# Layer norms of the second batch and of the s branch moved in small pieces into the attention loop, first projections put between the first norms

## The chip, the cores and the metric

The kernel runs on one core of one Trainium2 chip, in one launch. The metric is the device time of that launch in microseconds, the median of several runs. All tensors are float32. Engine names are those of the profile: PE is TensorE (PEld its weight loads), DVE is VectorE, ACT is ScalarE, POOL is GpSimd, SP is SyncE. ACT and SP also issue DMAs here (ACTq and SPq).

## The reference, cut to what matters

The input x has two batches of 2048 tokens with 256 features. It is normalised once, and the result xn goes into two branches: s, an attention over all 2048 tokens with 16 heads of 16, to which a second layer norm of xn is added; and g, two layers of windowed attention with a gated feed-forward. The output is x + s * silu(ffn(xn)).

```python
xn = _layernorm(x)                        # no weights: (x - mean) / sqrt(var + 1e-5)
# s branch
q, k, v = split(xn @ W_qkv.T)             # 16 heads of 16
attn = softmax(q @ k.T * scale + spatial_bias)    # bias on tokens 1..256 only
s = (attn @ v) @ W_proj.T + b_proj + _layernorm(xn) * ln_gamma + ln_beta
# spatial_bias: -0.1 * dist / max(dist) over 256 centres
g = silu(ffn(xn))                         # depth 2, windows of 128 tokens
out = x + s * g
```

## The kernel before

The program runs in three stages, one after the other: `norms`, `global_attention`, `ffn_branch`.

`norms` goes through eight chunks of 512 tokens, four to a batch, each held as four tiles of 128 tokens by 256 features. For each chunk it loads x (SP), takes mean and variance of each tile with a BATCH_NORM_STATS and a BATCH_NORM_AGGREGATE instruction (L92 and L93, DVE), takes the root on ACT (L95) and the reciprocal on DVE (L96), and writes the normalised tiles to `xn` (L106, four TENSOR_SCALAR). TensorE transposes the chunk into two banks `pt` (L112) and ACT copies them to `xA[b]` (L113), the transposed activations that all later projections read. Then the same statistics are taken of `xn`, and the result is written to `s_all` (L117, DVE), multiplied by gamma (L120, POOL) and increased by beta plus b_proj (L121, POOL). `s_all` is the accumulator of s; the attention adds its output to it.

`spatial_bias` computes the bias of 257 rows from the centres: five small DVE operations and a root on ACT for each of three row groups, a maximum over all partitions on POOL (L158), and a scaling (L160 to L166).

`global_attention` is written in manual order: every engine executes its instructions in the order in which the program emits them. The 4 groups of 4 heads, 2 batches and 4 query chunks make 32 units. Three kinds of pieces run through PE:

- P pieces (`max_piece`, L280): the scores of 128 queries against 512 keys for one head, of which DVE takes only the maximum (L283, `mx`).
- S pieces (`score_piece`, L316): the scores transposed, with the maximum already subtracted through an added row; ACT takes the exponential (L322). In the first query chunk of a group (qc == 0) DVE adds the bias to the first 257 rows (L320).
- V pieces (`sum_piece`, L335): the sums of exponentials times values; ACT copies the bank out (L344), POOL adds it to the running sum `o` (L345).

P pieces and V sums take their PSUM banks from a ring of four (`p`), S pieces and everything else from another ring of four (`s`). The written order of one period, four key tiles of one unit, is the list `PATTERN`; in it X stands for one piece of other work: the next group's projections (`prep_qk` L232, `prep_v` L247), the `augment` of a unit (L293), or the closing steps of a unit (`sums` L352, `normalize` L364, `project` L374). A unit has four periods; the loop runs 130 of them.

Before the loop, the projections of the first group run as one block (13 pieces of `prep_pieces(0)`), and then 80 P pieces alone (the lead), since the maxima of a whole unit have to be known before its first S piece. Each P piece in the lead needs one DVE maximum.

`ffn_branch` has its own pools and starts when the attention is done. It is not touched.

DMA order: SP issues the x chunks and the centres; ACT issues the weights wq, wk, wv, wp, ones and the three rows ln_gamma, ln_beta, b_proj. DMAs share eight completion semaphores in turn; an issue waits until the previous DMA on its semaphore has landed.

Of the kernel before, what the change touches and what calls it, by code (L numbers as in the profile page):

```python
# [11 lines left out]
F32 = mybir.dt.float32  # L12
# [6 lines left out]
P = 128  # L19
NT = N // P  # L20
CH = 512
# [16 lines left out]
def gated_recurrent_kernel(ctx: ExitStack, tc: tile.TileContext, t: dict, out: bass.AP):  # L38
# [28 lines left out]
    with tc.tile_pool(name="s", bufs=1) as sp:  # L67
        s_all = sp.tile([P, B * NT, D], F32, name="s_all")
        norms(tc, t, xA, s_all, ident, eps_t, x_ch)
        global_attention(tc, t, xA, s_all, s_out, ident)  # L70
# [3 lines left out]
def norms(tc, t, xA, s_all, ident, eps_t, x_ch):  # L74

    nc = tc.nc
    with tc.tile_pool(name="ln", bufs=2) as lp, tc.tile_pool(name="ln1", bufs=1) as lp1, tc.tile_pool(
        name="ln_ps", bufs=4, space=PSUM
    ) as lps:
        gam = lp1.tile([P, D], F32, name="gam")  # L80
        nc.scalar.dma_start(gam, t["ln_gamma"][None, :].to_broadcast([P, D]))
        bet = lp1.tile([P, D], F32, name="bet")
        nc.scalar.dma_start(bet, t["ln_beta"][None, :].to_broadcast([P, D]))
        bpr = lp1.tile([P, D], F32, name="bpr")
        nc.scalar.dma_start(bpr, t["b_proj"][None, :].to_broadcast([P, D]))
        nc.vector.tensor_add(bet, bet, bpr)

        def stats(src, c, tag):
            mv = lp.tile([P, TPC, 2], F32, tag=f"mv{tag}", name=f"mv{tag}_{c}")
            for i in range(TPC):  # L90
                st = lp.tile([P, 6], F32, tag=f"st{tag}", name=f"st{tag}_{c}_{i}", bufs=4)
                nc.vector.bn_stats(st, src[:, i, :])  # L92
                nc.vector.bn_aggr(mv[:, i, :], st)  # L93
            rs = lp.tile([P, TPC], F32, tag=f"rs{tag}", name=f"rs{tag}_{c}")
            nc.scalar.activation(rs, mv[:, :, 1], AF.Sqrt, bias=eps_t)  # L95
            nc.vector.reciprocal(rs, rs)  # L96
            return mv, rs

        for c in range(B * NCH):
            b, cc = divmod(c, NCH)  # L100
            xt = lp.tile([P, TPC, D], F32, tag="xt", name=f"xt_{c}", bufs=3)
            nc.sync.dma_start(xt, x_ch[c])
            mv, rs = stats(xt, c, "a")
            xn = lp.tile([P, TPC, D], F32, tag="xn", name=f"xn_{c}")
            for i in range(TPC):
                nc.vector.tensor_scalar(  # L106
                    xn[:, i, :], xt[:, i, :], mv[:, i, 0:1], rs[:, i : i + 1], ALU.subtract, ALU.mult
                )
            for k in range(2):
                pt = lps.tile([P, CH], F32, tag="pt", name=f"pt_{c}_{k}")  # L110
                for i in range(TPC):
                    nc.tensor.transpose(pt[:, i * P : (i + 1) * P], xn[:, i, k * P : (k + 1) * P], ident)  # L112
                nc.scalar.copy(xA[b][:, k, 1 + cc * CH : 1 + (cc + 1) * CH], pt)  # L113
            mv, rs = stats(xn, c, "b")
            sl = s_all[:, c * TPC : (c + 1) * TPC, :]
            for i in range(TPC):
                nc.vector.tensor_scalar(  # L117
                    sl[:, i, :], xn[:, i, :], mv[:, i, 0:1], rs[:, i : i + 1], ALU.subtract, ALU.mult
                )
            nc.gpsimd.tensor_mul(sl, sl, gam[:, None, :].to_broadcast([P, TPC, D]))  # L120
            nc.gpsimd.tensor_add(sl, sl, bet[:, None, :].to_broadcast([P, TPC, D]))  # L121


def spatial_bias(tc, t, pool):


    nc = tc.nc
    bias = pool.tile([P, 2, NC_SP], F32, name="bias")
    bias_last = pool.tile([1, NC_SP], F32, name="bias_last")
    with tc.tile_pool(name="sb", bufs=1) as sp:  # L130
        cb = sp.tile([P, NC_SP, 2], F32, name="cb")
        nc.sync.dma_start(
            cb.rearrange("p n c -> p (n c)"),
            t["centers"].rearrange("n c -> (n c)")[None, :].to_broadcast([P, 2 * NC_SP]),
        )
        cp = sp.tile([P, 3, 2], F32, name="cp")
        nc.gpsimd.memset(cp, 0.0)
        nc.sync.dma_start(cp[1:P, 0, :], t["centers"][0 : P - 1, :])
        nc.sync.dma_start(cp[:, 1, :], t["centers"][P - 1 : 2 * P - 1, :])
        nc.sync.dma_start(cp[0:1, 2, :], t["centers"][2 * P - 1 : 2 * P, :])  # L140
        dy = sp.tile([P, NC_SP], F32, name="dy")
        for kt in range(3):
            rows = P if kt < 2 else 1
            d = bias[:, kt, :] if kt < 2 else bias_last
            nc.vector.tensor_scalar(d, cb[:rows, :, 0], cp[:rows, kt, 0:1], None, ALU.subtract)
            nc.vector.tensor_mul(d, d, d)
            nc.vector.tensor_scalar(dy[:rows], cb[:rows, :, 1], cp[:rows, kt, 1:2], None, ALU.subtract)
            nc.vector.tensor_mul(dy[:rows], dy[:rows], dy[:rows])
            nc.vector.tensor_add(d, d, dy[:rows])
            nc.scalar.activation(d, d, AF.Sqrt)  # L150
        nc.vector.memset(bias[0:1, 0, :], 0.0)
        mx = sp.tile([P, 1], F32, name="mx")
        nc.vector.tensor_reduce(mx, bias.rearrange("p k n -> p (k n)"), AX.X, ALU.max)
        mx1 = sp.tile([1, 1], F32, name="mx1")
        nc.vector.tensor_reduce(mx1, bias_last, AX.X, ALU.max)
        nc.vector.tensor_max(mx[0:1], mx[0:1], mx1)
        mxa = sp.tile([P, 1], F32, name="mxa")
        nc.gpsimd.partition_all_reduce(mxa, mx, P, ReduceOp.max)  # L158
        on = sp.tile([P, 1], F32, name="on")
        nc.vector.tensor_scalar(on, mxa, 1e-6, -0.1, ALU.is_gt, ALU.mult)  # L160
        co = sp.tile([P, 1], F32, name="co")
        nc.vector.tensor_scalar_max(co, mxa, 1e-6)
        nc.vector.reciprocal(co, co)
        nc.vector.tensor_mul(co, co, on)
        nc.vector.tensor_scalar_mul(bias, bias, co)
        nc.vector.tensor_scalar_mul(bias_last, bias_last, co[0:1])  # L166
    return bias, bias_last
# [5 lines left out]
    "S0 S3 P1 P2 S0 P3 V V P2 P0 S3 S1 P1 P0 S3 S2 P1 S0 S2 P3 X P3 P0 S1 S2 X S1 P0 P2 S3 S1 S0 P2 P3 V V P1 S2"  # L173
# [7 lines left out]
def global_attention(tc, t, xA, s_all, s_out, ident):  # L181
# [6 lines left out]
    with ExitStack() as ctx:  # L188
        cp = ctx.enter_context(tc.tile_pool(name="ga_c", bufs=1))
        bias, bias_last = spatial_bias(tc, t, cp)  # L190
# [12 lines left out]
        negm = [cp.tile([P, TPC * GH, HP], F32, name=f"negm{i}") for i in range(2)]  # L203
        for m in negm:
            nc.gpsimd.memset(m, 0.0)
        ctx.enter_context(tc.manual_schedule())

        units = [(b, g, qc) for b in range(B) for g in range(NG) for qc in range(NCH)]
        groups = [(b, g) for b in range(B) for g in range(NG)]
# [779 lines left out]
```

## Time and profile before

| what | value |
|---|---|
| median of 3 runs | 3884.55 us (3881.63 to 3889.24) |
| profiled execution | 3884.26 us, of which the span is 3882.5 us |
| busy in the span | PE 92%, DVE 60%, ACT 53%, POOL 30% |
| first P piece starts | 118.03 us |
| first maximum of the lead (L283) starts | 119.19 us |
| end of the lead, first S piece (L316) starts | 176.59 us |
| one unit of the loop | 59.1 us (59.16 us from 793.57 to 852.73) |
| DMA | mean 10 GB/s over the span |

The page gives one execution, in microseconds from the start of the span. "Busy tenths" are 40 equal slices of 97 us. The chain is the sequence of work that ended last, followed back from the end. Matmul rows count each float32 matmul twice, since it is done in two passes with a weight load each.

### The profile page before, as it was taken

What the parts mean: (1) busy time and instruction counts of PE and PEld (TensorE: products, weight loads), DVE (VectorE), ACT (ScalarE), POOL (GpSimd) and SP (SyncE); (2) the same over time, 40 slices, a digit from 0 to 9 for tenths busy, and PEclk for the clock granted to TensorE, in tenths of its full rate; (3) what the DMA queues carried; (4) which work ended last, traced back from release to release, by engine and by line L of the source; (5) the groups of instructions that cost most, each with busy time, mean ns of one, the idle gap of its engine ahead of it and who ended that gap; (6) DMA issues with size and microseconds to landing.
All of it is one profiled execution on the core that took longest, in us unless ns stands there. A gap on an engine that the chain in (4) does not pass through costs nothing.

```text
span 3882.5 us, 56277 instructions
## 1 busy us (share of the span) xinstructions
PE 3564.7 (92%) x21856; PEld 1688.3 (43%) x21856; DVE 2334.0 (60%) x4894; ACT 2063.8 (53%) x4170; POOL 1156.3 (30%) x978
## 2 busy tenths in 40 slices
PE   2999999999999999999996778888989999999998
PEld 1534334334343343434432444444444445555554
DVE  8767777777777777777751444545444444444442
ACT  1166666666666666666663344444444444444452
POOL 4011111111111111111113544445444435454441
PEclk9699999999999999999997899999999999999999
DMA  2000000000000000000002000000000000000001
GB/s 72 4 1 1 1 1 1 1 1 1 12 6 7 1 1 1 1 1 1 1 12 79 1 6 1 6 1 6 1 22 6 1 28 9 17 17 17 17 9 44
DMA packets 26172, 40.44 MB, mean 10 GB/s; under 512 B 3806, under 2 KB 19122, under 8 KB 25906
## 3 DMA queue, kind: packets, MB, share of 16 engines
q1 hardware_dynamic: 24466, 34.08, 2.6%
q8 instruction: 172, 2.82, 0.3%
q10 hardware_dynamic: 1440, 2.77, 0.2%
q14 instruction: 94, 0.77, 0.1%
HBM read 28.46 MB, written 8.39 MB: 9 GB/s over the span
## 4 chain that ended last, share of the span: by engine, by line
PE 76%; DVE 11%; ACT 5%; POOL 5%; issue 2%; DMA 1%; ACTq 0%; POOLq 0%; SPq 0%; DVEq 0%
PE pm L280 16%; PE po L335 12%; PE ps L316 11%; PE pg L757 7%; PE pp L552 6%; PE po L689 4%; DVE mx L283 3%; PE px L704 3%; PE pz L800 2%; POOL sm L654 2%; PE pw L668 2%; PE px L374 2%; PE pt L598 2%; ACT sm L645 2%; PE pp_wk L232 2%
## 5 line engine op out<-in xcount | busy, mean ns | idle before, releaser
L283 DVE TENSOR_REDUCE mx<-pm 128x1 f32<-128x512 f32 x2048 | 1285.6, 683 | 450.9 <-PE ps L316 429.9
L322 ACT ACTIVATE e<-ps 128x512 f32<-128x512 f32 x2048 | 1059.4, 607 | 466.2 <-PE ps L316 345.0
L280 PE MATMUL pm<-kT,qT 32*128 32x512 f32 x4096 | 1148.8, 639 | 0.8 <-DVE mx L283 0.8
L316 PE MATMUL ps<-qa,kT 32*128 32x512 f32 x4096 | 1116.5, 627 | 5.7 <-ACT e L322 4.8
L345 POOL TENSOR_TENSOR o<-o,part 128x512 f32<-128x512 f32 x224 | 283.5, 1266 | 1580.6 <-ACT part L344 1580.6
L280 PEld LDWEIGHTS pm<-kT,qT 32*128 32x128 f32 x4096 | 432.4, 188 | 435.4 <-DVE mx L283 338.5
L335 PE MATMUL po<-e,v 128*32 128x512 f32 x4096 | 492.5, 598 | 0.0
L316 PEld LDWEIGHTS ps<-qa,kT 32*128 32x128 f32 x4096 | 390.9, 183 | 154.6 <-ACT e L322 62.5
L576 POOL TENSOR_TENSOR rot<-rot,swp 128x512 f32<-128x512 f32 x128 | 162.4, 1269 | 797.5 <-DVE swp L575 757.7
L552 PE MATMUL pp<-wqkv,xA 128*128 128x512 f32 x768 | 379.9, 618 | 14.4 <-DMA wqkv<-in_wqkv_dram 14.4
L757 PE MATMUL pg<-hc,w 128*128 128x512 f32 (+1 forms) x768 | 379.8, 629 | 0.0
L645 ACT ACTIVATE sm<-sm,wmx 128x256 f32<-128x256 f32 (+1 forms) x512 | 250.4, 490 | 171.9 <-DVE wmx L636 171.2
L654 POOL TENSOR_TENSOR sm<-sm,wls 128x512 f32<-128x512 f32 (+1 forms) x256 | 254.2, 1014 | 26.6 <-DVE wls L651 23.7
L335 PEld LDWEIGHTS po<-e,v 128*32 128x32 f32 x4096 | 106.9, 109 | 348.1 <-DVE mx L283 187.4
L573 DVE TENSOR_TENSOR rot<-pp,rt 128x512 f32<-128x512 f32 x128 | 88.5, 691 | 248.7 <-ACT sqq L567 230.4
L585 POOL TENSOR_TENSOR rn<-rn,mhalf 128x8 f32<-128x8 f32 x128 | 210.8, 1647 | 55.4 <-DVE rn L584 55.4
L344 ACT COPY part<-po 128x512 f32<-128x512 f32 x224 | 131.0, 585 | 167.0 <-PE po L335 167.0
L689 PE MATMUL po<-pT,v 128*64 128x128 f32 x1984 | 159.3, 301 | 55.8 <-DVE pT L675 55.8
L552 PEld LDWEIGHTS pp<-wqkv,xA 128*128 128x128 f32 x768 | 138.7, 197 | 154.3 <-issue 141.2
L668 PE MATMUL pw<-ident,sm 128*128 128x128 f32 x992 | 150.0, 288 | 60.6 <-POOL sm L654 59.7
L675 DVE COPY pT<-pw 128x512 f32<-128x512 f32 (+1 forms) x128 | 84.8, 672 | 195.5 <-PE pw L668 195.4
L757 PEld LDWEIGHTS pg<-hc,w 128*128 128x128 f32 (+1 forms) x768 | 132.9, 187 | 142.0 <-issue 141.3
(136 smaller groups left out, 3795.8 us busy)
## 6 DMA issues: line engine op xcount, KB each, us to landing
xt<-in_x_dram SPq DMA_DIRECT2D x8, 512.0 KB, 3.7
s_out<-s_all SPq DMA_DIRECT2D x8, 512.0 KB, 2.6
rt<-in_rot_dram SPq DMA_DIRECT2D x16, 256.0 KB, 4.6
s<-s_out SPq DMA_DIRECT2D x16, 256.0 KB, 3.4
x<-in_x_dram SPq DMA_DIRECT2D x16, 256.0 KB, 3.5
out_dram<-y SPq DMA_DIRECT2D x16, 256.0 KB, 2.2
wqkv<-in_wqkv_dram SPq DMA_DIRECT2D x4, 768.0 KB, 8.3
w<-in_w_dram SPq DMA_DIRECT2D x4, 682.0 KB, 5.5
```

The costliest lines, as they stand in the source:

```text
L280: nc.tensor.matmul(ps, qT[rows, q0 : q0 + P], kT[rows, c * CH : (c + 1) * CH], start=True, stop=True)
L283: nc.vector.tensor_reduce(mxs[n][:, i * GH + j, c : c + 1], ps, AX.X, ALU.max)
L316: nc.tensor.matmul(ps, kT[rows, kt * P : (kt + 1) * P], qas[n][rows, :], start=True, stop=True)
L322: nc.scalar.activation(e, ps, AF.Exp)
L335: nc.tensor.matmul(pos[n][j * HP : (j + 1) * HP, :], v[:, kt, j * HP : (j + 1) * HP], es.pop((n, kt, j)), start=(kt % 2 == 0), stop=(kt % ...
L345: nc.gpsimd.tensor_add(os[n], os[n], part)
L552: nc.tensor.matmul(ps, xA[b][:, k, at : at + P], W["qkv"][:, k, n * INNER : (n + 1) * INNER], start=(k == 0), stop=(k == 1),)
L645: nc.scalar.activation(sm[:, x, lo:], sm[:, x, lo:], AF.Exp, scale=-1.0, bias=mx[:, hb, r, x : x + 1], accum_out=ls[:, hb, r, x : x + 1],)
L654: nc.gpsimd.tensor_mul(sm, sm, ls[:, hb, r, :, None].to_broadcast([P, 2, 2 * P - lo]))
L668: nc.tensor.transpose(ps[:, x, pa, :], S["sm"][hb, r][:, x, pa * P : (pa + 1) * P], ident)
L689: nc.tensor.matmul(S["po"][r * HD2 : (r + 1) * HD2, c, :], kvs[l, b, kt, "v"][:, h * HD2 : (h + 1) * HD2], S["pT", hb, r][:, x, pa, :], st ...
L757: nc.tensor.matmul(ps[:mw], W["1"][:, k, at : at + mw], hc[:, k, :], start=(k == 0), stop=(k == 1))
```

## The change

The function `norms` is gone, and its work is in `global_attention` as pieces.

1. Batch 0's first norm: load, statistics, root (still on ACT), application and transposes of a chunk are emitted chunk by chunk before the loop. Between them stand a step of `spatial_bias`, now a generator that yields between its steps, and the projections of group 0 for the chunk before (`prep_qk` for wk and wq, then `prep_v`). The rest of `spatial_bias` and the addition of b_proj to beta follow after the last projection and before the lead.
2. The norm of s (`s_pieces`) and batch 1's first norm (`xn_pieces` of chunks 4 to 7) are split into 80 pieces in the list `aside`, in the order: s of batch 0 (24 pieces), xn of batch 1 (32), s of batch 1 (24). A new letter N in `PATTERN`, three times a period, executes one of them. N stands after the first V pair, after the first X, and after the second V pair.
3. In the loop the inverse root is a power on POOL (`inv_std`, an add and a pow of 128x4). The normalised tile is written into `s_all` itself, the transposes read it there (`turn_over`), and the norm of s is done in place by two SCALAR_TENSOR_TENSOR instructions of DVE for each tile, which contain gamma and beta. The two POOL instructions of a chunk (L120, L121) are gone.
4. wq, wk, wv, wp and ones are issued at the start of the program, before gamma, beta and b_proj. x has two buffers in place of three; the temporaries of `spatial_bias` share the buffers of `e`.

```diff
-        norms(tc, t, xA, s_all, ident, eps_t, x_ch)
-        global_attention(tc, t, xA, s_all, s_out, ident)
+        global_attention(tc, t, xA, s_all, s_out, ident, eps_t, x_ch)
...
-            mv, rs = stats(xn, c, "b")
-            sl = s_all[:, c * TPC : (c + 1) * TPC, :]
-            for i in range(TPC):
-                nc.vector.tensor_scalar(
-                    sl[:, i, :], xn[:, i, :], mv[:, i, 0:1], rs[:, i : i + 1], ALU.subtract, ALU.mult
-                )
-            nc.gpsimd.tensor_mul(sl, sl, gam[:, None, :].to_broadcast([P, TPC, D]))
-            nc.gpsimd.tensor_add(sl, sl, bet[:, None, :].to_broadcast([P, TPC, D]))
...
-    "S0 S3 P1 P2 S0 P3 V V P2 P0 S3 S1 P1 P0 S3 S2 P1 S0 S2 P3 X P3 P0 S1 S2 X S1 P0 P2 S3 S1 S0 P2 P3 V V P1 S2"
+    "S0 S3 P1 P2 S0 P3 V V N P2 P0 S3 S1 P1 P0 S3 S2 P1 S0 S2 P3 X N P3 P0 S1 S2 X S1 P0 P2 S3 S1 S0 P2 P3 V V N P1 S2"
...
+        def stats(src, mv, tiles):
+            for i in tiles:
+                st = p2.tile([P, 6], F32, tag="st", name="st", bufs=4)
+                nc.vector.bn_stats(st, src[:, i, :])
+                nc.vector.bn_aggr(mv[:, i, :], st)
+
+        def inv_std(mv, rs):
+            nc.gpsimd.tensor_add(rs, mv[:, :, 1], ep4)
+            nc.gpsimd.tensor_tensor(rs, rs, mhalf, ALU.pow)
...
+            def root():
+                if b:
+                    inv_std(h["mv"], h["rs"])
+                else:
+                    nc.scalar.activation(h["rs"], h["mv"][:, :, 1], AF.Sqrt, bias=eps_t)
+                    nc.vector.reciprocal(h["rs"], h["rs"])
+
+            def apply(tiles):
+                for i in tiles:
+                    nc.vector.tensor_scalar(
+                        sl[:, i, :], h["x"][:, i, :], h["mv"][:, i, 0:1], h["rs"][:, i : i + 1],
+                        ALU.subtract, ALU.mult,
+                    )
+
+            def turn_over(k):
+                pt = bank(f"pt_{c}_{k}")
+                for i in range(TPC):
+                    nc.tensor.transpose(pt[:, i * P : (i + 1) * P], sl[:, i, k * P : (k + 1) * P], ident)
+                nc.scalar.copy(xA[b][:, k, 1 + cc * CH : 1 + (cc + 1) * CH], pt)
+
+            return [
+                load, lambda: stats(h["x"], h["mv"], (0, 1)), lambda: stats(h["x"], h["mv"], (2, 3)), root,
+                lambda: apply((0, 1)), lambda: apply((2, 3)),
+            ], [lambda: turn_over(0), lambda: turn_over(1)]
...
+            def first():
...
+                stats(sl, h["mv"], (0, 1))
+
+            def rest():
+                stats(sl, h["mv"], (2, 3))
+                inv_std(h["mv"], h["rs"])
+
+            def apply(i):
+                x = sl[:, i, :]
+                nc.vector.scalar_tensor_tensor(x, x, h["mv"][:, i, 0:1], gam, ALU.subtract, ALU.mult)
+                nc.vector.scalar_tensor_tensor(x, x, h["rs"][:, i : i + 1], bet, ALU.mult, ALU.add)
+
+            return [first, rest] + [(lambda i=i: apply(i)) for i in range(TPC)]
...
-        for f in prep_pieces(0):
-            f()
+        open_group(0)
+        sb = spatial_bias(tc, t, cp, p2, tag="e", bufs=20)
+        firsts = [xn_pieces(c) for c in range(NCH)]
+        for c in range(2):
+            firsts[c][0].pop(0)()
+        for c in range(NCH + 1):
+            if c < NCH:
+                if c + 2 < NCH:
+                    firsts[c + 2][0].pop(0)()
+                for f in firsts[c][0] + firsts[c][1]:
+                    f()
+                next(sb)
+            if c:
+                prep_qk(0, "wk", c - 1)
+                prep_qk(0, "wq", c - 1)
+                prep_v(0, c - 1)
+        bias, bias_last = list(sb)[-1]
+        nc.vector.tensor_add(bet, bet, bpr)
+        aside = [f for c in range(NCH) for f in s_pieces(c)]
+        for c in range(NCH, 2 * NCH):
+            own, turns = xn_pieces(c)
+            aside += own + turns
+        aside += [f for c in range(NCH, 2 * NCH) for f in s_pieces(c)]
...
+                elif op == "N":
+                    if aside:
+                        aside.pop(0)()
```

In `spatial_bias` the operations are the same and only the `yield` statements are new: one after its DMAs, one after each of the three row groups, and one after the maximum on POOL.

## The prediction

> **What bounds the kernel now.** I read the busy tenths first, then the chain of waits, then the timeline of the first 200 us, and last the DVE timeline of two periods of the loop.
>
> ```profile
> PE   2999999999999999999996778888989999999998
> DVE  8767777777777777777751444545444444444442
> PEclk9699999999999999999997899999999999999999
> ```
>
> PE is full in every slice of the attention but the first (97 us), where DVE is full. So the norms are a stage of their own in which PE waits. The chain names what holds it:
>
> ```profile
> 74.81 4.43 DVE xn L106 x2
> 93.97 10.12 PE pp_wk L232 x16
> 104.09 6.87 PE pp_wq L232 x16
> 110.96 7.14 PE pv L247 x64
> 119.93 54.76 PE pm L280 x136
> ```
>
> DVE's norms until about 88 us, then the block of projections, then the lead. From about 195 us the chain is PE almost throughout. Within the norms, the timeline shows what one chunk costs:
>
> ```profile
> 14.90 1.36 DVE L106 TENSOR_SCALAR xn<-xt,mva,rsa 128x256 f32<-128x256 f32 x4
> 27.31 4.77 DVE L106 TENSOR_SCALAR xn<-xt,mva,rsa 128x256 f32<-128x256 f32 x4
> 28.95 2.34 POOL L121 TENSOR_TENSOR s_all<-s_all,bet 128x1024 f32<-128x1024 f32 x1
> 96.66 0.34 PEld L232 LDWEIGHTS pp_wk<-xA,wk 128*128 128x128 f32 x1 [0.52 <-issue]
> 100.92 0.19 PEld L232 LDWEIGHTS pp_wk<-xA,wk 128*128 128x128 f32 x1 [0.24 <-issue]
> ```
>
> The same four TENSOR_SCALAR took 1.36 us while POOL was idle and 4.77 us beside POOL's multiply and add. The weight loads of the projections came every 0.86 us (0.34 and 0.52 idle) until 100 us, every 0.43 us after: PE ran at half pace for its first 6.1 us. In the loop DVE looks like this (a period with projections, then one with `project`):
>
> ```profile
> 242.22 1.89 DVE L283 TENSOR_REDUCE mx<-pm 128x1 f32<-128x512 f32 x3 [0.17 <-PE pm L280]
> 245.15 3.68 DVE L283 TENSOR_REDUCE mx<-pm 128x1 f32<-128x512 f32 x6 [1.04 <-PE ps L316]
> 250.61 1.29 DVE L283 TENSOR_REDUCE mx<-pm 128x1 f32<-128x512 f32 x2 [1.79 <-PE ps L316]
> 253.64 2.48 DVE L283 TENSOR_REDUCE mx<-pm 128x1 f32<-128x512 f32 x4 [1.74 <-PE ps L316]
> 257.40 0.69 DVE L283 TENSOR_REDUCE mx<-pm 128x1 f32<-128x512 f32 x1 [1.28 <-PE ps L316]
> ...
> 339.32 1.29 DVE L283 TENSOR_REDUCE mx<-pm 128x1 f32<-128x512 f32 x2 [0.34 <-PE ps L316]
> ```
>
> DVE idles 1.04 us after the first V pair (the first N), 1.28 us after the second (the third N), and after the first X (the second N) 1.79 us beside a projection, but only 0.34 us beside `project`.
>
> **The head, step by step.** The sum is made against the profiled execution, 3884.26 us (1.8 us outside the span), 0.3 us under the median. The first maximum stands at 119.19 us; I build its new place.
>
> 1. Chunks 0 and 1. x landed at 4.87 us; I take 5.5, since wq and wk now share the DMAs. ACT issues bpr behind its semaphore predecessor wq, so ACT's table load waits for wq; I place that inside the statistics. Statistics of four tiles: 4 x (397 + 155 ns, L92 and L93) = 2.2 us; table load 1.28, root 0.30, reciprocal 0.18 and the gaps: 2.0; application 1.36 to 1.4. That is 11.1 us. Chunk 1: statistics 2.2, root and reciprocal 0.8, application 1.4, and 1.3 for the tail of its transposes: 16.8 us. The 5.2 us for which DVE waited on b_proj at L86 are gone, because that addition now comes late.
> 2. Projections of one chunk: 8 passes of 0.43 us (wk, wq) and 16 of 0.114 (7.31 us for 64, L247) = 5.3 us at full pace, about 10.6 at half pace. With a first 6 us at half pace as at 94 us: 8.3 us. First block: 25.1 us.
> 3. The next chunk's statistics stand behind the addition for v (L251, 0.69 us) in DVE's order, and that waits for the projections. So between two blocks lie 0.7 + 2.2 + 0.8 + 1.4 + 1.3 = 6.4 us without dense PE work. Chunk 2 to 31.5, its follower block to 39.8, chunk 3 to 46.2, then two blocks together, 8.3 + 5.3, to 59.8 us. The bias steps (5 operations of 0.34 to 0.41 us) stand on DVE before L251 and lie under the blocks, if the centres have landed. Their DMAs are behind chunk 2's load on SP, which waits for chunk 0's application (11 us); the slowest such DMA took 8 us, so they land by about 20 us and are done before 25.1. If they land later, the whole head shifts with them.
> 4. After the last block DVE has the v addition 0.7, the end of the bias (93.24 to 98.58 us before, 5.4 us) and the b_proj addition 0.42 before it takes a maximum: first maximum at 66.3 us. PE fills four banks and waits. Before, the first maximum stood 1.2 us after the projections; now 6.5.
>
> Gain: 119.19 - 66.3 = 52.9 us. The lead (80 maxima, 56.7 us) is unchanged.
>
> [...] The trace has 6.1 us, and its PEclk column says 1.00 there, so I go by the pace of the weight loads: 66.3. If the gap of 6.4 us does not cool PE, blocks two and three save 6.0 us: 60.3. If only the last block ran at full pace, three blocks cost 10.6: 73.2.
>
> **The loop.** 80 pieces at three a period last 27 periods.
>
> - `turn_over`: 8 pieces of four transposes. The like piece L293 takes 0.59 us on the chain, L364 0.66: 8 x 0.65 = 5.2 us, all on PE's path. Their copies (0.59 us, ACT) lie in ACT's idle time; ACT is 65% busy there. Of the 16 transposing pieces before, none was hidden by PE work, so this is half of them moved onto a full PE.
> - DVE: 24 pairs of statistics of 1.1 us = 26.5; 16 applications of 0.34 = 5.4; 64 SCALAR_TENSOR_TENSOR. That operation in SBUF is not in the trace: the nearest row is the TENSOR_TENSOR 128x256 of `spatial_bias`, 408 ns, so 26.1. Together 58 us. At the first and third N a piece of 0.7 to 1.1 us fits the idle 1.04 and 1.28 us. At the second N it fits in one period of four; in the others it is about 0.5 us too long, and V waits for the banks behind it. Some 13 such pieces with DVE work: 6 us.
> - The first period of a group with qc == 0 has 12 bias additions on DVE. A unit with them took 61.4 us (852.73 to 914.17) against 59.16: DVE is the limit there and every piece counts. Two such periods (units 0 and 4) lie in the 27: 2 x 2.5 = 5 us.
> - POOL: 12 roots, each an add and a pow; L585 (128x8) 1.65 us. POOL is about 16% busy in the loop. `apply` comes an N later, 3.8 to 6 us; behind a part addition (0.8 to 2.1 us after V) the root is ready 4.0 us after V, so at most a few tenths on DVE. Bounds: 0, or 12 x 1.65 = 20 if nothing else hides it; I take 1. What is queued behind a waiting `apply` on DVE are the maxima, and PE waits for those.
> - DMA: the four x loads of batch 1 are behind nothing but each other on SP, whose next need is `s_out` of unit 12; 0.
>
> [...] The row: L106 beside POOL, 1046 ns in the mean against 340. [...] By the row, 80 x 0.7 = 56 us; [...] in the written order POOL's addition starts 0.8 us after a V pair and the N piece right at its end, so most miss it. I take 1 us on the path, and keep 0 to 56.
>
> Loop: 5.2 + 6 + 5 + 1 + 1 = 18 us. Sum: 3884.3 - 52.9 + 18 = about 3849 us.
>
> **The rivals.**
>
> - *Slots hide all.* PE stays warm (60.3) and only transposes and bias periods cost, 10 us: 3884.3 - 58.9 + 10 = 3835. For: the idle stretches repeat to 0.01 us. Against: the chain's `mx x6` of 3.66 us in each unit, where DVE already leads. 0.2.
> - *The head is late.* Cold blocks (73.2) and centres or weights some 5 us late, loop as forecast: 3884.3 - 41 + 18 = 3861. For: ACT and SP issues wait for semaphore predecessors, 2 MB of weights compete with x. 0.2.
> - *No measurable change.* Late head (-41) and all of DVE's 58 us at the share that the bias additions paid (2.3 of 4.9 us, 47%: 27), with 5 + 5 and some root waits: about 3882. 0.04.
> - *Slower[...].* DVE's in-place operations behave in the loop as L106 did beside POOL: 80 x 0.7 = 56 on top of 18: 3884.3 - 53 + 74 = 3905. It decides from a mean wait of 0.44 us an operation (35 us over 80). For: the row is there. Against: POOL worked without pause then, and is 16% busy in the loop. 0.06.
>
> **The numbers.** The forecast case, 0.5, gives 3849, by itself 3841 to 3857. The range reaches over the first two rivals with the ends of head and loop: 3828 to 3871, leaving out about 2 in 10. A measurement can tell 0.2%, some 8 us. Faster 0.89, same 0.05, slower 0.06.
>
> **What would show it.** First maximum at 60 to 73 us, with DVE's bias end and b_proj before it. Gaps of about 6 us between the projection blocks ended by DVE's application. The lead as long as before. The first 27 periods together longer by about 18 us, later ones unchanged; units 0 and 4 longest. SCALAR_TENSOR_TENSOR near 0.41 us[...]. If the early periods lengthen by over 1.5 us each, the slots do not hold and I am wrong on the loop; if the first maximum comes after 80 us, on the head.

## The result and the profile after

The changed kernel takes 3843.51 us (median of 4 runs, 3842.92 to 3844.01); beside it the kernel before took 3885.88 us. The ratio is 0.9891, with a 95% interval of 0.9876 to 0.9907. The forecast was 3849 us, with a range of 3828 to 3871. The profiled execution of after took 3843.72 us, and its span is 3841.9 us, 40.6 us less than that of before.

The busy tenths of after, in the three rows that were shown of before:

```profile
PE   7999999999999999999995789888898999999998
DVE  5888887777777777777732445444544444545442
PEclk7899999999999999999997899999999999999999
```

In the first slice PE has gone from 2 tenths to 7 and DVE from 8 to 5. In slices 2 to 6, where the small pieces now are, DVE stands at 8 where it was at 6 or 7. The chain of waits of after (start, length, engine, operation) begins with a DMA, and no DVE row of the norms is among its longest pieces any more:

```profile
1.75 8.06 DMA wq<-in_wq_dram
62.90 55.28 PE pm L312 x152
...
634.72 3.66 DVE mx L315 x6
```

The line numbers are those of after: P pieces L312 with the maximum L315, S pieces L348, V pieces L367, projections L264 and L279, the addition for v L283, the application of the first norm L211, its transposes L219.

**The head.** The timeline of after, from the first statistics to the second block of projections (start, length, engine, instruction, and in brackets the idle time before it and what ended that):

```profile
6.85 0.18 DVE L184 BATCH_NORM_AGGREGATE mv<-st 128x2 f32<-128x6 f32 x1
9.83 0.34 ACTq L164 DMA_DIRECT2D bpr<-in_b_proj_dram  x1
10.26 1.28 ACT L206 ACT_TABLE_LOAD   x1 [10.26 <-DMA wq<-in_wq_dram]
12.10 1.38 DVE L211 TENSOR_SCALAR s_all<-xt,mv,rs 128x256 f32<-128x256 f32 x4
18.75 3.49 PE L264 MATMUL pp_wk<-xA,wk 128*128 128x512 f32 x4
21.31 0.34 PEld L264 LDWEIGHTS pp_wq<-xA,wq 128*128 128x128 f32 x1 [0.52 <-issue]
22.51 0.19 PEld L264 LDWEIGHTS pp_wq<-xA,wq 128*128 128x128 f32 x1 [0.24 <-issue]
25.78 0.69 DVE L283 TENSOR_TENSOR v<-pv,ones 128x512 f32<-128x512 f32 x1 [5.25 <-PE pv L279]
29.18 1.39 DVE L211 TENSOR_SCALAR s_all<-xt,mv,rs 128x256 f32<-128x256 f32 x4
31.74 3.62 PE L264 MATMUL pp_wk<-xA,wk 128*128 128x512 f32 x4
35.16 0.34 PEld L264 LDWEIGHTS pp_wq<-xA,wq 128*128 128x128 f32 x1 [0.52 <-issue]
36.26 0.19 PEld L264 LDWEIGHTS pp_wq<-xA,wq 128*128 128x128 f32 x1 [0.24 <-issue]
```

The statistics are done at 7.03 us, but ACT stands until 10.26 behind the issue of `bpr`, which waits for wq: 3.2 us lost (in before the issues of `cb`, L132, and `cp`, L139, waited 1.1 us each for vecs and b_row). Then the first block runs from 18.75 to 25.78, where the addition for v follows its last matmul. From 18.54 to 21.98 us a weight load comes every 0.86 us (0.34 and 0.52 idle), after that every 0.43 us: half pace, then full pace. Before the second block lie 6.0 us, in which DVE adds, takes the statistics of the next chunk and applies them. The second block begins at half pace again, and so does the third.

The end of the head, again in the timeline of after:

```profile
57.81 0.69 DVE L283 TENSOR_TENSOR v<-pv,ones 128x512 f32<-128x512 f32 x1 [4.53 <-PE pv L279]
60.53 0.15 DVE L111 TENSOR_SCALAR on<-mxa 128x1 f32<-128x1 f32 x1 [0.55 <-POOL mxa L108]
61.84 0.41 DVE L433 TENSOR_TENSOR bet<-bet,bpr 128x256 f32<-128x256 f32 x1
62.17 2.47 DVE L315 TENSOR_REDUCE mx<-pm 128x1 f32<-128x512 f32 x4
```

The first maximum starts at 62.17 us, where it was 119.19: 57.0 us earlier. It stands 4.5 us after the last projection. The lead has kept its length within half a microsecond (`qa`, the DVE instruction at its end, starts at 119.26 us; it was 175.84): 56.6 us are left there.

**The loop.** Those 56.6 us become 40.6 at the end: the loop gives back 16.0 us. The chain's rows `mx x6` show where: from 634.72 us on (675.38 in before) every such row stands 40.6 us ahead, so the loss lies entirely in the periods with pieces. Taken from the starts of the V pairs in both traces (a V pair is two V pieces written side by side, 16 matmuls on PE), it is 4.4 us in the first period, 2.7 in the period at 384 us (unit 4, the other one with a bias addition), 4.2 for the eight transposing pieces, 1.0 in the seven periods after the first, which hold the pieces of s of batch 0, and the other 3.7 us in small amounts over the rest. This is DVE in one of the quiet periods of after:

```profile
165.78 0.42 DVE L183 BATCH_NORM_STATS2 st<-s_all 128x6 f32<-128x256 f32 x1
...
166.76 0.18 DVE L184 BATCH_NORM_AGGREGATE mvs<-st 128x2 f32<-128x6 f32 x1
167.65 1.29 DVE L315 TENSOR_REDUCE mx<-pm 128x1 f32<-128x512 f32 x2 [0.71 <-PE ps L348]
170.68 2.48 DVE L315 TENSOR_REDUCE mx<-pm 128x1 f32<-128x512 f32 x4 [1.74 <-PE ps L348]
173.08 0.48 DVE L243 SCALAR_TENSOR_TENSOR s_all<-s_all,mvs,gam 128x256 f32<-128x256 f32 x1
173.66 0.48 DVE L244 SCALAR_TENSOR_TENSOR s_all<-s_all,rss,bet 128x256 f32<-128x256 f32 x1
174.44 0.69 DVE L315 TENSOR_REDUCE mx<-pm 128x1 f32<-128x512 f32 x1 [0.29 <-PE ps L348]
```

The idle 1.79 us at the second N has become 1.16 us of statistics (two pairs) and 0.71 idle, the 1.28 us at the third N two instructions and 0.29 idle; the 1.74 us between them, where no N stands, is as it was. Such a period costs next to nothing, 1.0 us in seven. The first period is another matter. The first two V pairs of the loop on PE, and two windows of after (us; busy and count of PE, PEld, DVE, ACT, POOL; granted clock; DMA share; GB/s):

```profile
137.45 3.64 PE L367 MATMUL po<-e,v 128*32 128x512 f32 x16
143.13 1.92 PE L367 MATMUL po<-e,v 128*32 128x512 f32 x16
...
120.00:135.00 15.00, 12.16 (x53) 5.24 (x53) 12.69 (x32) 5.64 (x11) 1.26 (x2) 0.84 0.01 2
135.00:145.00 10.00, 10.00 (x58) 2.88 (x58) 5.73 (x10) 5.10 (x10) 0.00 (x0) 0.68 0.00 1
```

Up to 135 us DVE is the busiest engine and PE waits; right after it PE is busy without pause but at a granted clock of 0.68, and the first V pair takes 3.64 us in place of 1.92. So of the 4.4 us some 1.9 fall on this pair and the pieces behind it and are clock; the other 2.5 are lost before it, where DVE leads.

### The profile page after: what moved, and what is told of

Same layout as the page of the kernel before. It is cut to its first block, busy times and chain, and to the rows that moved or that the text cites. A ratio compares the mean times of both kernels' runs of the same rounds, so it can differ in the third digit from the quotient of the medians.

```text
span 3841.9 us, 56247 instructions
## 1 busy us (share of the span) xinstructions
PE 3571.6 (93%) x21856; PEld 1691.0 (44%) x21856; DVE 2331.6 (61%) x4914; ACT 2060.8 (54%) x4158; POOL 1133.1 (29%) x988
## 4 chain that ended last, share of the span: by engine, by line
PE 77%; DVE 10%; ACT 5%; POOL 5%; issue 2%; DMA 1%; ACTq 0%; POOLq 0%; SPq 0%; DVEq 0%
PE pm L312 16%; PE po L367 12%; PE ps L348 11%; PE pg L813 7%; PE pp L608 6%; PE po L745 4%; DVE mx L315 3%; PE px L760 3%; PE pz L856 2%; POOL sm L710 2%; PE pw L724 2%; PE px L406 2%; PE pt L654 2%; ACT sm L701 2%; PE pp_wk L264 2%
## 5 line engine op out<-in xcount | busy, mean ns | idle before, releaser
L315 DVE TENSOR_REDUCE mx<-pm 128x1 f32<-128x512 f32 x2048 | 1285.4, 683 | 409.5 <-PE ps L348 385.0
L312 PE MATMUL pm<-kT,qT 32*128 32x512 f32 x4096 | 1151.3, 640 | 4.5 <-DVE mx L315 4.5
L348 PE MATMUL ps<-qa,kT 32*128 32x512 f32 x4096 | 1120.3, 627 | 8.2 <-ACT e L354 7.4
L312 PEld LDWEIGHTS pm<-kT,qT 32*128 32x128 f32 x4096 | 432.7, 188 | 435.5 <-DVE mx L315 322.9
L367 PE MATMUL po<-e,v 128*32 128x512 f32 x4096 | 495.8, 602 | 0.0
L348 PEld LDWEIGHTS ps<-qa,kT 32*128 32x128 f32 x4096 | 392.7, 184 | 161.4 <-ACT e L354 66.8
L367 PEld LDWEIGHTS po<-e,v 128*32 128x32 f32 x4096 | 107.4, 109 | 350.1 <-DVE mx L315 186.6
```

The costliest lines, as they stand in the source:

```text
L312: nc.tensor.matmul(ps, qT[rows, q0 : q0 + P], kT[rows, c * CH : (c + 1) * CH], start=True, stop=True)
L315: nc.vector.tensor_reduce(mxs[n][:, i * GH + j, c : c + 1], ps, AX.X, ALU.max)
L348: nc.tensor.matmul(ps, kT[rows, kt * P : (kt + 1) * P], qas[n][rows, :], start=True, stop=True)
L367: nc.tensor.matmul(pos[n][j * HP : (j + 1) * HP, :], v[:, kt, j * HP : (j + 1) * HP], es.pop((n, kt, j)), start=(kt % 2 == 0), stop=(kt % ...
```

## Experiments: the head

Up to the section on all together, each kernel is the changed kernel with one edit. The profiled time of after, 3843.72 us, is what they are held against; where a run has a single time, that is named. Places in the trace (the first maximum, `qa`, V pairs, the last row `mx x6` of the chain, at 1937.73 in after) tell what the total can't.

**no_interleave.** The norms first, then the projections in one block:

```diff
-        for c in range(NCH + 1):
-            if c < NCH:
...
+        for c in range(NCH):
+            if c + 2 < NCH:
+                firsts[c + 2][0].pop(0)()
+            for f in firsts[c][0] + firsts[c][1]:
+                f()
+            next(sb)
+        for c in range(NCH):
+            prep_qk(0, "wk", c)
+            prep_qk(0, "wq", c)
+            prep_v(0, c)
```

> One part undone: the four first norms run one after the other, then the four projection blocks together; all else as in the changed kernel (first P piece there at 57.7 us, 3843.5 us). Theory A (the gain comes from taking work out of the head; putting projections between the norms is worth little, since DVE's addition for v holds the next chunk's statistics behind each block): DVE needs about 12.1 us to the first application and then 3 x 6.4 us, so the transposes end near 33 us, four blocks take 3.3 + 4 x 5.3 = 24.5 us, first P piece at about 58 us, time 3841 to 3846. Theory B (the interleaving carries a good part of the gain): first P piece at 68 to 75 us, time 3853 to 3860.

One run: 3840.08 us. The first maximum stands at 59.21 us and `qa` at 116.38, 2.9 us ahead of after. Only the first of the four blocks is slow (32.16 to 38.98, 6.8 us), the others take 5.2. So putting projections between the norms, a part of point 1 of the change, costs about 3 us as it is done: each gap brings a start at half pace, 1.7 to 2.1 us lost, and that is more than what the overlap saves. The gain of the head must then come from the other parts: the norms of s and of batch 1 are out of it, and wk and wq are issued at the start, where ACT issued them at 88 us before. These two were not tried apart.

**norm_ahead.** The next chunk's load, statistics, root and application are emitted before the block of projections and before its addition for v, which on DVE stood ahead of them:

```diff
-        for c in range(NCH + 1):
+        for c in range(-1, NCH + 1):
+            if c + 1 < NCH:
...
+                for f in firsts[c + 1][0]:
+                    f()
+            if 0 <= c < NCH:
+                for f in firsts[c][1]:
                     f()
                 next(sb)
-            if c:
+            if c > 0:
                 prep_qk(0, "wk", c - 1)
```

> The norm of the chunk after next is emitted before the projections of a chunk, so that neither DVE's addition for v nor ACT's copies of q and k stand before it; nothing else changes. Theory A (the 6.0 us between two projection blocks are DVE's queue order, and PE cools down in them): the blocks follow each other with only transposes (1.3 to 2.2 us) between, only the first is at half pace, first P piece at about 46 us in place of 57.7, time about 3832. Theory B (the gaps come from DMA arrival or from ACT, or PE cools down anyway): first P piece at 54 to 58 us, time 3839 to 3844.

One run: 3831.76 us, 12.0 below after's profiled run; `qa` stands at 107.46, 11.8 ahead. The timeline of norm_ahead:

```profile
22.80 0.33 PEld L264 LDWEIGHTS pp_wq<-xA,wq 128*128 128x128 f32 x1 [0.52 <-issue]
24.09 0.19 PEld L264 LDWEIGHTS pp_wq<-xA,wq 128*128 128x128 f32 x1 [0.24 <-issue]
26.93 0.69 DVE L283 TENSOR_TENSOR v<-pv,ones 128x512 f32<-128x512 f32 x1 [1.62 <-PE pv L279]
27.61 1.88 PE L264 MATMUL pp_wk<-xA,wk 128*128 128x512 f32 x4
50.36 1.87 DVE L315 TENSOR_REDUCE mx<-pm 128x1 f32<-128x512 f32 x3
```

The second block's first four matmuls follow the first block within 0.7 us and take 1.88 us where they took 3.62. The gap is gone and with it the cold start: what made it was the order of emission, in which the addition for v stood before the next statistics on DVE and the copies of q and k before the next root on ACT; the edit moves both. The interleaving that cost 3 us is then 8 us better than no_interleave, once DVE has the next chunk ready.

**rows_late.** gamma, beta and b_proj are issued by SP after the projections, so ACT has nothing queued behind wq:

```diff
-        nc.scalar.dma_start(gam, t["ln_gamma"][None, :].to_broadcast([P, D]))
...
                 prep_v(0, c - 1)
+        nc.sync.dma_start(gam, t["ln_gamma"][None, :].to_broadcast([P, D]))
+        nc.sync.dma_start(bet, t["ln_beta"][None, :].to_broadcast([P, D]))
+        nc.sync.dma_start(bpr, t["b_proj"][None, :].to_broadcast([P, D]))
```

> The DMAs of gamma, beta and b_proj are issued by SP after the projections' emission instead of by ACT at the start; nothing else changes. Theory A (ACT's first root waited 3.2 us, from 7.0 to 10.26 us, only because b_proj's issue stood before it and waited for wq): first root at about 8.4 us instead of 11.55, first P piece 3 us earlier at about 54.6, time about 3840.5. Theory B (something later, such as the landing of the second x chunk or of the weights, holds the head as well): first P piece less than 1 us earlier, time 3842.5 to 3844.

One run: 3840.11 us. The timeline of rows_late:

```profile
7.01 1.28 ACT L203 ACT_TABLE_LOAD   x1 [7.01 <-DVE mv L181]
8.85 1.38 DVE L208 TENSOR_SCALAR s_all<-xt,mv,rs 128x256 f32<-128x256 f32 x4
```

ACT now waits for the statistics, and the application comes 3.25 us earlier; `qa` is 3.5 us ahead of after. The 3.2 us read off the chain were on the path in full.

**tail_in_lead.** The end of the bias and the b_proj addition are put between the maxima of the lead:

```diff
-        bias, bias_last = list(sb)[-1]
-        nc.vector.tensor_add(bet, bet, bpr)
...
+            if at == 3:
+                next(sb)
+            if at == 6:
+                bias, bias_last = next(sb)
+            if at == 8:
+                nc.vector.tensor_add(bet, bet, bpr)
```

> The end of the spatial bias and the addition of b_proj to beta are emitted between the maxima of the lead (after its 16th, 28th and 36th) instead of before it; nothing else changes. Theory A (these operations are 3.8 us of DVE on the path before the lead, while in the lead DVE idles 0.36 us in every 2.85): first maximum at about 58.8 us instead of 62.17, end of the lead about 3 us earlier, time about 3840.5. Theory B (the lead is bound by DVE, so that what is moved into it is paid there): first maximum at 58.8 us but the end of the lead unchanged, time 3843 to 3844.

One run: 3840.59 us. The first maximum follows the last projection by 1.05 us and stands at 59.15, but the lead is longer by the moved work, since DVE leads there too: `qa` is 1.7 us ahead, in a run in which wq landed 0.5 us later. Counted from the last addition for v, the first maximum comes 3.3 us earlier than in after and `qa` 2.0: so 2.0 us are kept. Of these 0.55 are DVE's wait on POOL, and 1.1 are three of the pauses of 0.37 us that DVE makes after every four maxima in the lead: the moved work fills them, and only the rest of it lengthens the lead.

## Experiments: the loop

**skip_bias.** No piece in the periods with a bias addition:

```diff
-                    if aside:
+                    if aside and at % (NG * NCH):
                         aside.pop(0)()
```

> N pieces are left out of the two periods whose S pieces carry the spatial bias (period 0 and 16); the six pieces run later. In the changed kernel the head's gain falls there by 4.4 and 2.7 us, and the first V pair of each lasts 3.6 us instead of 1.92. Theory A (the pieces stretch the bias period, PE falls to half pace in it, and the slow V pair is a second price): without them the V pairs last 1.92 us again, and of the 7.1 us all but about 1 us comes back: 3836.5 to 3838.5. Theory B (only DVE's own work counts, PE's pace is set by the lead before it): V stays at 3.6 us, 3 to 3.5 us come back: 3840 to 3841.

One run: 3838.98 us; the last row `mx x6` is at 1933.30, 4.4 us ahead of after, of which 1.1 are from the head. The first two V pairs of the loop take 1.92 us, and the second comes 18.9 us after `qa` in place of 23.9: that period's loss is undone. In the period at 375 us it is not: no piece stands there, and yet the V pair takes 2.89 us. The windows of skip_bias:

```profile
135.00:145.00 10.00, 10.00 (x72) 3.91 (x68) 8.23 (x18) 6.74 (x13) 1.27 (x1) 1.00 0.00 1
375.00:380.00 5.00, 5.00 (x28) 1.15 (x29) 2.29 (x4) 2.37 (x5) 0.00 (x0) 0.66 0.00 0
```

So in period 0 the half clock goes with the pieces. In unit 4's period the bias alone, after periods filled with pieces, is enough. Nor do all the pieces have to go: in two_n (below) two pieces stand in each of these periods, and only the one after X is missing; period 0 then loses 0.5 us, unit 4's (where one of the two is only a load) nothing, and the V pairs take 1.92 us.

**n_misplaced.** Three N a period still, but at other places of the order, after P1, S1 and S3:

```diff
-    "S0 S3 P1 P2 S0 P3 V V N P2 ... X N P3 ... V V N P1 S2"
+    "S0 S3 P1 N P2 S0 P3 V V P2 P0 S3 S1 N P1 ... P2 S3 N S1 ..."
```

> The three N of a period stand inside the stretches in which DVE takes maxima without a pause (after the third op, after the fourth op behind the first V pair, and after the sixth op behind the second X) instead of behind the V pairs and the first X; same pieces, same number. Theory A (the place matters: DVE's idle 1.0 to 1.8 us behind V and X are what hides the pieces, elsewhere PE waits for the banks that the late maxima hold): the loop loses well over the 16 us of the changed kernel, time 3852 to 3870. Theory B (DVE is 75% busy in the loop and any place will do, since the queue catches up at the next pause): 3842 to 3846.

One run: 3852.76 us. `qa` is within 0.3 us of after's, the last `mx x6` 8.1 us later: the loop's cost goes from 16.0 to about 24. The same pieces at the same rate cost half as much again there. Of the 8 us about 3 belong to transposing pieces, which hold no DVE work: by the starts of the V pairs three of the eight cost 1.63 us each at the new place, where a piece cost 0.4 to 0.6 in after. The place matters, but even so they cost far less than the 58 us of DVE time that was summed for them.

**two_n.** The second N, that after X, is taken out, so that the pieces last 40 periods:

```diff
-    "... S2 P3 X N P3 ..."
+    "... S2 P3 X P3 ..."
```

> The second N of a period (behind the first X, where DVE idles only 0.3 us beside most X pieces) is taken out of the pattern; the same 80 pieces then take 40 periods at two a period. Theory A (the losses outside the bias periods and the transposes come from that place): the marks of the periods lose only at the transposes (about 0.5 us each) and in the bias periods 0, 16 and 32, two pieces each; 3839 to 3842. Theory B (the pieces cost the same wherever DVE takes them, so only their number counts): 3843 to 3845.

One run: 3838.12 us. The last `mx x6` is at 1926.87, 10.9 us ahead of after (0.6 of it from the head). The loop's cost thus falls from 16.0 to 5.7, about the price of the transposes. But the total gains only 5.6 us: 5.9 us are lost from that row to the DMA of `sc`, in the last units, which no edit touches, and the ffn stage gives 0.6 back. The chains show the same pieces there, of two_n

```profile
2008.95 7.24 PE ps L348 x18
2016.18 3.57 PE po L367 x16
```

and of after:

```profile
2017.05 6.29 PE ps L348 x17
2026.24 1.90 PE po L367 x16
```

A V pair takes 3.57 us where others take 1.9, and the granted clock is 0.83 from 2000 to 2020 us of two_n; in after it is 1.00 from 1960 to 2020. This stretch at half clock costs some 3 us, and another, at a V piece of 3.08 us at 1962.91, the like.

**turn_double and turn_double_again.** Each transposing piece of the loop is done twice:

```diff
-                pt = bank(f"pt_{c}_{k}")
+                for r in range(1 + b):
+                    pt = bank(f"pt_{c}_{k}_{r}")
...
```

> Each of the eight transposing pieces in the loop does its four transposes and the copy twice, into two banks; nothing else changes. Theory A (these pieces lie on PE's path, 4.2 us for eight in the changed kernel by the marks of the periods): another 4 to 5.5 us, 3847.5 to 3849. Theory B (they are hidden by waits of PE that are there anyway): less than 1 us, 3843 to 3844.5.

> The kernel with doubled transposing pieces once more, several executions: its first look gave 3857.1 us, 13.6 more than the changed kernel, of which 3.8 lay in the periods with the pieces and the rest in the last two units and in the feed-forward stage, whose instructions are the same. Theory A (that rest is PE's clock falling to half for a few microseconds in some executions, at a place that shifts with the start): the fastest runs are at 3847 to 3848.5, some higher by about 5. Theory B (the doubled pieces cause it): all runs at 3855 to 3859.

The first run took 3857.1 us, and the same kernel again 3856.08 (3851.59 to 3856.87; ratio 0.9932, 0.9916 to 0.9949). From `qa` to the last `mx x6` it is 4.0 us longer than after in both profiles: 0.5 us for each of the eight pieces of four transposes, on the path in full. The rest lies behind that row in unchanged code. In the first profile the last units take 5.3 us more and the ffn stage another 4.4, in the second profile, the quickest of its kernel, the last units take 3.1 more; each shows a V pair of 3.57 us, at 2003.73 and at 2029.22. Neither theory had that. What the traces show of such stretches stands in the last section.

## Experiments: all together

**combined.** norm_ahead, rows_late, tail_in_lead and skip_bias, and the projections of the second group in the last thirteen steps of the lead, where DVE leads and PE waits:

```diff
+        early = prep_pieces(1)
...
+            if at >= 7:
+                early.pop(0)()
```

> Norms ahead of the projections, the three rows issued by SP, the end of the bias inside the lead, no N in the bias periods, and the second group's projections (12 pieces, 1.9 to 2.0 us of PE each) emitted in the lead instead of in the loop's X places. If the savings add (head 12 + 3.3 + 3, bias periods 6, projections 12 x 1.95 = 23 less 4 us for DVE's v additions in the lead): about 3800 us. If the lead, bound by DVE and with PE at half pace, pays for the projections (12 x 1.9 x 2 on PE at half pace, 45 us, in a lead whose PE is busy without a pause): the 23 us come back as cost and the time is 3820 to 3830.

3814.43 us (3812.53 to 3824.67; ratio 0.9816, 0.9799 to 0.9832): short of the 3800 that was expected if the savings add, and better than the 3820 to 3830 of the other case. A lead step with a projection took 3.35 us where one without took 2.85. In the early periods, where no projection fills an X any more, DVE was busy for 36.6 us of 40 (from 160 us on).

**combined_two.** The same with the projections spread over the whole lead, three in five steps, and with two N a period:

> The combination again, with the second group's 12 projections spread over the lead from its first steps (in three of five steps, in place of one in each of the last thirteen), and two N a period in place of three. Theory A (a step of four maxima takes DVE 2.5 us, and PE at full pace about 1.1 us for the P pieces and 1.9 us for a projection, so that spread out they fit under DVE, and PE stays at full pace): the lead takes 54 to 58 us instead of 68.7, time 3798 to 3804. Theory B (PE falls to half pace in the lead anyway, and each projection costs 3.7 us there): lead 66 to 72 us, time 3808 to 3815.

3811.77 us (3810.65 to 3816.11; ratio 0.9819, 0.9805 to 0.9834). Spread out, half of the projections ran cold: for the four matmuls of one, four of the eight of q and k took 3.64 to 3.78 us and the other four 1.98, and the lead lasted 78 us. The loop with two N was better: from the first V pair to the last `mx x6` it took 1775 us, in combined 1787.

**combined_last.** The projections of combined, two N of combined_two:

> The first combination (second group's projections one a step in the last thirteen steps of the lead, where PE stayed at full pace from the second of them on) with two N a period in place of three. The first combination reached the first V pair at 125.5 us and the last unit but two at 1912.7; the second one, 134.9 and 1910.1. Theory A (the lead's and the loop's savings are independent): first V pair at 125 to 127 us, the mark at about 1901, time 3798 to 3806. Theory B (the loop's early periods were slow in the first combination because no projections stood in the X places, not because of the second N): mark at 1909 or later, time 3808 to 3814.

3801.42 us (3801.05 to 3804.08; ratio to before 0.9783, 0.9767 to 0.9800). The first V pair is at 124.05, the last `mx x6` at 1898.29, 1774 us later: the lead of combined and the loop of combined_two, so these two savings add up. This version is the fastest here, 83 us below before and 42 below the change as made. Its lead, in the windows and in PE's timeline:

```profile
50.00:70.00 20.00, 19.93 (x48) 11.21 (x46) 17.58 (x35) 0.00 (x0) 0.38 (x1) 0.50 0.00 0
70.00:90.00 20.00, 20.00 (x72) 6.92 (x71) 13.51 (x22) 3.94 (x6) 0.00 (x0) 0.97 0.00 1
...
68.00 3.50 PE L261 MATMUL pp_wk<-xA,wk 128*128 128x512 f32 x4
72.51 1.98 PE L261 MATMUL pp_wk<-xA,wk 128*128 128x512 f32 x4
```

With P pieces alone, matmuls of 32 rows, PE counts as busy for 19.93 of 20 us and yet has half the clock; one projection of 128 rows at half pace, and from the next on the clock stays up (0.97 in the mean of the window).

## Why the prediction was right, and where it was off

The mechanism was right: the head shrinks by the norms that leave it, the loop gives over a quarter of that back. 3884.3 - 56.6 + 16.0 gives 3843.7, against 3884.3 - 52.9 + 18. Both terms were off to the same side. Each was nearer than its parts: in the head an error of 2.4 us one way stands against three the other way, in the loop the bias periods were put too low and the rest too high. That much was luck.

- *Chunks 0 and 1, step 1: off by 2.4 us, too early.* ACT's wait for wq was seen, but "I place that inside the statistics" was wrong: ACT was held for 3.2 us after them. The first application ended at 13.5 us rather than 11.1. rows_late shows the term.
- *Half pace, step 2: the mis-sized term.* 3.0 us were put on each cold block from the 6.1 us before; the three blocks took 7.0 to 7.4 us rather than 8.3, a loss of 1.7 to 2.1 us each. The first block of norm_ahead lost 2.2. The 6.1 us were measured at another start and did not carry over. From the block's start to full pace it is 6.1 us in before (93.97 to 100.05), 3.2, 3.9 and 4.2 in after (18.75 to 21.98, 31.74 to 35.64, 45.07 to 49.29). In after the starts lie 12.99 and 13.33 us apart and the rises 13.66 and 13.65; what sets the moment of the rise was not shown. This put the head 3.2 us too late.
- *Gaps, step 3: right.* 6.0 us where 6.4 were summed, and the block behind each gap began at half pace. The cause, the addition for v ahead of the statistics in DVE's order, is shown by norm_ahead as far as emission order goes; ACT's copies moved with it. The centres had landed by 18.5 us, as assumed.
- *The tail, step 4: 4.5 rather than 6.5 us.* The 5.4 us taken from before held 2.33 us of waiting on POOL's all-reduce; in after that wait is 0.55 us. POOL had been free for 7.18 us before it in before too (the profile gives "issue" for that time), so why the wait was longer there stays open.
- *Transposes: right.* 4.2 us measured where 5.2 were summed. That they are not hidden at all is shown by turn_double.
- *Second N and bias periods: right together, wrongly split.* 6 and 5 us were given. The two bias periods took 7.1, of which much is half clock, which no step had; the second N beside a projection took nothing (the fit "in one period of four" was too strict for statistics of 1.16 us), and the sum of all that is neither transposes nor bias is 4.7 us, where 6 + 1 + 1 stood.
- *Roots on POOL: right.* These are the groups of after in the loop, by form (busy, mean ns, then idle before):

```profile
L244 DVE SCALAR_TENSOR_TENSOR s_all<-s_all,rss,bet 128x256 f32<-128x256 f32 x32 | 16.1, 502 | 1.7
L243 DVE SCALAR_TENSOR_TENSOR s_all<-s_all,mvs,gam 128x256 f32<-128x256 f32 x32 | 15.0, 468 | 0.0
L188 POOL TENSOR_TENSOR rss<-rss,mh 128x4 f32<-128x4 f32 x8 | 8.2, 1023 | 0.6
```

  L244 is the one that needs the root; all its waiting is 1.7 us in 32 instructions.
- *DVE beside POOL: right to size it small.* 468 and 502 ns against the 408 of the nearest row: 64 instructions are 4.9 us longer in all, most of it within idle slots. The rival that ended slower needed a mean wait of 0.44 us, and these rows rule it out. The trace also tells what the difference is: 49 of the 64 ran while POOL did nothing, and they took 473 to 486 ns all the same, so the step from 408 is not POOL's. Of the 15 that ran beside POOL 12 took 391 to 487 ns and three 643 to 710: that is about 0.5 us for all 64, where 1 us was put.

Of the other rivals, "slots hide all" was right for the quiet periods and wrong for the bias periods; "the head is late" was right on ACT's wait, 3.2 us of it, and wrong on the cold blocks. "No measurable change" needed 41 us in the head and 37 or more lost in the loop; it was 56.6 and 16.0.

## What to carry to other kernels

- Interleaving two stages pays only if the engine that feeds the next step has it ready before the current block ends. Look in that engine's order for what stands ahead of it and waits for the block; here one addition of 0.69 us made gaps of 6 us and after each a start at half pace of 3.9 and 4.2 us; the order without them was worth 12 us.
- Idle slots of an engine can be filled at almost no cost where they are as long as the piece, and the same pieces cost half as much again a few instructions further on. Where that engine already leads, count the slots: in the two bias periods here two pieces cost 0.5 us at most, three 4.4 and 2.7.
- When a part of the profile at half clock is used as a price, ask whether its length belongs to that stage: measure the pace at other starts of the same kind, since here it took 3.2 to 6.1 us for the clock to rise.

## What was not expected of the hardware

- PE's granted clock was 0.50 in a stretch where PE was busy for 19.93 of 20 us with matmuls of 32 rows (lead of combined_last), and 0.97 once projections of 128 rows stood between them. By the record PE is full in both. The leads of before (140 to 175 us, PE busy for 35.00 of 35) and of after (80 to 110 us, 30.00 of 30), P pieces alone as well, have 0.50 too. No run changed the rows alone, so that they are the cause was not shown.
- One and the same bias period ran at full pace in one version and partly at half pace in others. That of unit 8 holds no piece in after, skip_bias, n_misplaced and combined_two. The first of its two v projections takes 2.05 us in after (at 620.54 us; the granted clock is 1.00 from 613.3 to 628) and in before, and 3.68, 3.32 and 3.49 in the other three, behind the same pause of 0.23 us. From V pair to V pair the period takes 14.53 us in before and 14.54 in after, 16.17 in skip_bias and 16.13 in n_misplaced. What decides it was not shown.
- The stretches in the last two units are of this kind too. There S pieces run alone for 6 to 7 us. Such a row took 6.29 us, and the V pair behind it 1.85, in combined_last (from 1977.62 us), n_misplaced (2025.14) and turn_double_again (1982.81); it took 7.24, and the V pair 3.57, in two_n (2008.95) and turn_double_again (2021.98).
- Behind the first period of the loop, in which PE waits for DVE, PE ran at half pace for some microseconds though it did not wait any more: 3.50 to 3.64 us for the first V pair of the loop in after, no_interleave, norm_ahead, rows_late, tail_in_lead, turn_double and turn_double_again, and 2.72 in combined_last, which has no piece in that period; 1.92 in skip_bias and two_n. It is 1.92 in n_misplaced too, but there the clock was 0.50 from 110 to 135 us and 0.94 in the mean from 135 to 145, with the pair at 136.66.
- Half-clock stretches in the last two units, where nothing was edited, moved totals by 3 to 6 us between versions (from the last `mx x6` to the DMA of `sc`: 103.9 us in after and n_misplaced, 109.6 in combined, 109.8 in two_n). A difference of a few microseconds in this kernel has to be read from places in the trace, not from the total alone.
